# A recurrent spiking layer: TensorE's work of a time step gathered into two groups, each behind one wait

## The chip, the cores and the metric

The kernel runs on one core of a Trainium2 chip. The metric is the device time of one execution in microseconds (us), as the median of several runs. A core has five engines with instruction queues of their own: PE (TensorE, matrix products and transposes), DVE (VectorE), ACT (ScalarE), POOL (GpSimd) and SP (SyncE). They tell each other of finished work through semaphores: an instruction may wait for a semaphore to reach a value, and it may raise one when it has finished. DMA transfers raise semaphores too.

## The reference

A batch of 1024 sequences has 50 item numbers each. Every item has a row of 128 numbers in a table of 100,001 rows, and item 0 counts as a row of zeros. Per step t, the running sum of the rows is divided by min(t, length), normalized over the batch, and fed to a leaky neuron that fires at 1. The share of steps in which it fired, times the whole table transposed, is the output: 1024 x 100,001 scores.

```python
emb = emb_table.at[0].set(0.0)
prefix = jnp.cumsum(emb[seq], axis=1)
uF = prefix / denom[:, :, None]              # denom = min(t, length)
y = (uF - mean) * lax.rsqrt(var + BN_EPS) * gamma + beta   # mean, var over the batch
def step(v, x):
    v = v + (x - v) / TAU
    spike = atan_spike(v - V_TH)             # 1 where v >= V_TH
    return v - spike * V_TH, spike
_, spikes = lax.scan(step, v0, jnp.moveaxis(y, 1, 0))
scores = spikes.mean(axis=0) @ emb.T
```

## The kernel before

The kernel has two halves, and the order of the instructions of each engine is the order in which the program writes them.

**The scan** runs over the 50 steps. The 128 features lie on the partitions and the 1024 sequences along the free dimension, in two halves of 512 (h = 0 and 1)[...]. For step t, POOL gathers the 1024 rows with eight indirect DMAs of 128 rows (`gather`, L192 to L204) into a buffer `e`. A gather has its own one of eight DMA semaphores (the n-th of a step the n-th). Seven buffers take turns until step 42, three of them named `e` and four in the place where the second half's first two pairs of table slices will lie; the last seven steps use the three `e` buffers. `gathers` (L207) issues as many gathers as have a buffer whose earlier contents were read.

PE keeps the running sum of all rows in two PSUM banks, `pre[0]` and `pre[1]`. It adds a step by transposing the eight gathered blocks into them, four a bank (L313). `correct` (L269, matmuls on L271) subtracts row 0 of the table where the item is 0; it needs a small matrix `l` that ACT makes (`only`, L266). `counted` (L280, matmuls on L282) adds the spikes `s` of a step to two more banks, `sums`.

DVE scales each half of the sum to `uF` as soon as its four transposes are in (L322), takes statistics (L323, L333), finds the spikes of the step before (`s`, L343), and works out the normalization (L346 to L352). ACT applies it (L338, L356). DVE makes `negv` (L365) and the new potential `v` (L359). The scan's order on PE, for one step, is: four transposes of half 0, four of half 1, both corrections of the next step, both counts of the step before. In steps 42 and 44, `prepare` (L134) also transposes and splits the first two slices of the table, with a copy `hi` on ACT (L142) and a difference `lo` on DVE (L143). The last step takes its spikes with two DVE instructions ahead of `uF` (L307, L308).

**The product** (from L381) multiplies the counts, split into eight blocks of 128 sequences, by the table in slices of 1024 rows. The 36 slices that it needs first were fetched at the very start. Results go from PSUM through DVE (L472) and ACT (L474) to output buffers, and out by DMA from SP's queue: 409.6 MB.

Semaphores are set by the layer that records the program. Where instructions of one engine follow each other and only the last one's end has to be known, it may let one of them carry the increments of all. An instruction that must wait for more semaphores than it can hold gets wait instructions (EventSemaphore) in front of it.

Of the kernel before, what the change touches and what calls it, by code (L numbers as in the profile page):

```python
# [17 lines left out]
AF = mybir.ActivationFunctionType  # L18
ALU = mybir.AluOpType

P = 128
# [4 lines left out]
BANK = 512  # L26
# [8 lines left out]
def rec_kernel(  # L35
# [9 lines left out]
    nc = tc.nc  # L45
    B, T = seq.shape
    N, D = table.shape
    NB = B // P
# [18 lines left out]
    ident = const.tile([P, P], F32, tag="ident", name="ident")  # L67
# [10 lines left out]
    def pair(i):  # L78
        free.append([embp.tile([P, HALF], F32R, tag=f"{x}{i}", name=f"{x}_{i}") for x in ("hi", "lo")])
# [54 lines left out]
    def prepare(q, pt):  # L134
        turned(q, pt)
        split[q] = hi, lo = free.pop(0)
        hw = size(q)
        if hw % 2:
            nc.vector.memset(hi[:, hw : hw + 1].bitcast(F32), 0.0)
            nc.vector.memset(lo[:, hw : hw + 1].bitcast(F32), 0.0)  # L140
        vp, vh, vl = views(q, pt, hi, lo)
        nc.scalar.copy(vh, vp)  # L142
        nc.vector.tensor_tensor(vl, vp, vh.bitcast(F32), ALU.subtract)  # L143
# [18 lines left out]
    with ExitStack() as ph:  # L162
# [25 lines left out]
        slots += [f"e{(t - flat + 1) % 3}" for t in range(flat, T)]  # L188
        es = {}
        held = {}  # L190

        def gather(t):  # L192
            tag = slots[t]
            pool = gp if tag[0] == "e" else embp
            es[t] = pool.tile([P, B], F32, tag=tag, name=f"e_{t}")
            held[tag] = t
            for n in range(NB):
                nc.gpsimd.indirect_dma_start(  # L198
                    out=es[t][:, n * P : (n + 1) * P],
                    out_offset=None,  # L200
                    in_=table,
                    in_offset=bass.IndirectOffsetOnAxis(ap=idx[:, n, t : t + 1].bitcast(U32), axis=0),
                )
# [3 lines left out]
        def gathers(t):  # L207
            nonlocal to_gather
            while to_gather < T and held.get(slots[to_gather], -1) < t:
                gather(to_gather)  # L210
                to_gather += 1
# [4 lines left out]
        while slots[to_gather] != "e1":  # L216
            gather(to_gather)
            to_gather += 1
# [11 lines left out]
        r0n = once.tile([P, D], F32, tag="r0n", name="r0n")  # L230
# [3 lines left out]
        sel = once.tile([P, P // 2], F32, tag="sel", name="sel")  # L234
# [10 lines left out]
        rlen = once.tile([P, B], F32, tag="rlen", name="rlen")  # L245
# [14 lines left out]
        pre = [accp.tile([P, BANK], F32, tag=f"pre{h}", name=f"pre{h}") for h in range(B // BANK)]  # L260
        sums = [accp.tile([P, BANK], F32, tag=f"sums{h}", name=f"sums{h}") for h in range(B // BANK)]

        def only(t):

            l = sp.tile([P, D], F32R, tag="l", name=f"l_{t}")
            nc.scalar.activation(l, r0n, AF.Copy, scale=sel[:, t : t + 1])  # L266
            return l

        def correct(t, l):  # L269
            for h in range(B // BANK):  # L270
                nc.tensor.matmul(  # L271
                    pre[h],
                    lhsT=l,
                    rhs=zT[:, h * BANK : (h + 1) * BANK],
                    start=t == 0,
                    stop=False,
                    skip_group_check=True,
                )

        def counted(t, s):  # L280
            for h in range(B // BANK):
                nc.tensor.matmul(  # L282
                    sums[h],
                    lhsT=ident_h,
                    rhs=s[:, h * BANK : (h + 1) * BANK],
                    start=t == 0,
                    stop=t == T - 2,
                    skip_group_check=True,
                )
# [6 lines left out]
        halves = [slice(h * BANK, (h + 1) * BANK) for h in range(B // BANK)]  # L296
        v = None

        correct(0, only(0))
        l = only(1)  # L300
        for t in range(T):
            last = t == T - 1
            gathers(t)
            e = es.pop(t)
            if last:
                s = lp.tile([P, B], BF16, tag="s", name=f"s_{t - 1}")
                nc.vector.tensor_single_scalar(s, v, V_TH, ALU.is_ge)  # L307
                nc.vector.tensor_tensor(negv, s, v, ALU.subtract)  # L308
            uF = up.tile([P, B], F32, tag="uF", name=f"uF_{t}")
            bs = sp.tile([P, B // BANK, 6], F32, tag="bs", name=f"bs_{t}")  # L310
            for h, cs in enumerate(halves):
                for k in range(0, BANK, P):
                    nc.tensor.matmul(  # L313
                        pre[h][:, k : k + P],
                        lhsT=e[:, h * BANK + k : h * BANK + k + P],
                        rhs=ident,
                        start=False,
                        stop=last,
                        is_transpose=True,
                        skip_group_check=True,  # L320
                    )
                nc.vector.scalar_tensor_tensor(uF[:, cs], rlen[:, cs], 1.0 / (t + 1), pre[h], ALU.max, ALU.mult)  # L322
                nc.vector.bn_stats(bs[:, h, :], uF[:, cs])  # L323
            if not last:
                correct(t + 1, l)
            else:

                counted(t - 1, s)
                count = once.tile([P, B], F32, tag="zT", name="count")
                for h, cs in enumerate(halves):  # L330
                    nc.scalar.copy(count[:, cs], sums[h])
            mv = sp.tile([P, 2], F32, tag="mv", name=f"mv_{t}")
            nc.vector.bn_aggr(mv, bs.rearrange("p h s -> p (h s)"))  # L333


            r = sp.tile([P, 1], F32, tag="r", name=f"r_{t}")
            nc.scalar.activation(r, mv[:, 1:2], AF.Sqrt, bias=eps)  # L337
            nc.scalar.activation(uF, uF, AF.Identity, bias=mv[:, 0:1], scale=-1.0)  # L338


            if t and not last:
                s = lp.tile([P, B], BF16, tag="s", name=f"s_{t - 1}")
                nc.vector.tensor_single_scalar(s, v, V_TH, ALU.is_ge)  # L343
                counted(t - 1, s)

            nc.vector.reciprocal(r, r)  # L346
            q = sp.tile([P, 1], F32, tag="q", name=f"q_{t}")
            nc.vector.tensor_mul(q, r, r)
            nc.vector.scalar_tensor_tensor(q, mv[:, 1:2], BN_EPS, q, ALU.add, ALU.mult)
            nc.vector.tensor_scalar(q, q, -0.5, 1.5, ALU.mult, ALU.add)  # L350
            a = sp.tile([P, 1], F32, tag="a", name=f"a_{t}")
            nc.vector.tensor_scalar(a, q, r, hgb[:, 0:1], ALU.mult, ALU.mult)  # L352


            def x(vt, cs):
                nc.scalar.activation(vt, uF[:, cs], AF.Identity, bias=hgb[:, 1:2], scale=a)  # L356

            def step(vt, cs):
                nc.vector.scalar_tensor_tensor(vt, negv[:, cs], -0.5, vt, ALU.mult, ALU.add)  # L359

            if not last:
                vt = vp.tile([P, B], F32, tag=f"v{t % 2}", name=f"v_{t}")
                x(vt, whole)
                if t:
                    nc.vector.tensor_tensor(negv, s, v, ALU.subtract)  # L365
                step(vt, whole)
                v = vt
                if t + 2 < T:
                    l = only(t + 2)

                if t in (T - 8, T - 6):
                    q = (t - T + 8) // 2
                    pair(q)
                    prepare(q, vp.tile([P, HALF], F32, tag="v1", name=f"pt_{q}"))
# [15 lines left out]
        cs, vt, first = groups[0]  # L390
# [37 lines left out]
    for c, W in enumerate(WIDTHS):  # L428

        if c in (0, NARROW, MIDDLE):  # L430
# [3 lines left out]
            if c == 0:  # L434
                third = [op.tile([P, HALF], F32R, tag=x, name=x) for x in ("hi2", "lo2")]
                free.append(third)
                turns = [(op, f"o{k}", 2) for k in range(4)]
            elif c == NARROW:
                assert third in free
                free.remove(third)  # L440
                turns = [(op, f"o{k}", 3) for k in (2, 0, 1)]
            else:
                fourth = op.tile([P, 4, HALF], F32R, tag="pairs", name="pairs")
                free.extend((fourth[:, k, :], fourth[:, k + 1, :]) for k in (0, 2))
                turns = [(rowp, "rows2", 6), (rowp, "rows3", 6), (op, "o", 6)]
# [68 lines left out]
```

## Time and profile before

| | |
|---|---|
| median of 3 runs | 1676.47 us (1675.02 to 1677.37) |
| the profiled execution | 1672.07 us, of which the span in the trace is 1670.3 us |
| PE busy | 1111.4 us, 67% |
| DVE busy | 940.2 us, 56% |
| ACT busy | 630.7 us, 38% |
| POOL busy | 378.6 us, 23%, all of it in the first 586 us |
| DMA queue of the outputs (q1) | 428.77 MB |
| gathers (q0) | 26.24 MB in 400 indirect DMAs |
| first product of the second half | 604.34 us after the span's start |

All times in the text are us from the span's start unless it says otherwise. A busy time is the time in which an engine worked; a share of the span is a mean over both halves, so the halves have to be looked at apart. The start of a matmul is recorded, its end is modelled. The trace also holds the times at which each semaphore went up, though not every one of them, and each DMA packet. A row of a timeline gives the start, the duration, the engine, the line, the operation, what it writes and reads, and in brackets the engine's idle time before it and what ended that.

### The profile page before, as it was taken

Reading aid. Unit: us, or ns where it says so; the run is one execution under the profiler, and the core shown is the slowest. Engines: PE = TensorE matmul, PEld = TensorE weight load, DVE = VectorE, ACT = ScalarE, POOL = GpSimd, SP = SyncE. Lnnn points to the kernel's source line nnn. Section 1 sums busy time; section 2 is a strip of 40 time slices with the busy share of each in tenths; the row PEclk is TensorE's granted clock in tenths of the full one; section 3 lists DMA queues with packets and bytes.
Section 4 is the critical chain, followed back from the end, with each engine's and each line's share of the span. In section 5 each row is a group of like instructions: output and inputs, shape, how many; then the busy total and the mean of one; then the engine's idle time right before and its main releaser. Section 6 shows DMA issues by size and latency. Waiting matters only on the chain.

```text
span 1670.3 us, 12572 instructions
## 1 busy us (share of the span) xinstructions
PE 1111.4 (67%) x4548; PEld 830.0 (50%) x4548; DVE 940.2 (56%) x1161; ACT 630.7 (38%) x700; POOL 378.6 (23%) x406
## 2 busy tenths in 40 slices
PE   4113343434344479889988788878788888878785
PEld 2002121212222256666766666667666666666664
DVE  4225675657687875666655555555555554555553
ACT  2012232222232345545544444444444444444442
POOL 7766666667645600000000000000000000000000
PEclk9997555555555579999999999998999999999998
DMA  9511111111111149999999999999999999999998
GB/s 344 213 43 43 44 49 46 47 46 48 48 30 38 48 164 417 410 422 401 422 427 428 430 423 429 427 421 425 420 430 412 411 427 427 421 423 410 403 422 352
DMA packets 53691, 488.14 MB, mean 292 GB/s; under 512 B 11995, under 2 KB 12796, under 8 KB 32380
## 3 DMA queue, kind: packets, MB, share of 16 engines
q1 hardware_dynamic: 31984, 428.77, 61.1%
q0 software_dynamic: 12800, 26.24, 5.8%
q10 hardware_dynamic: 8844, 32.33, 4.9%
q8 instruction: 36, 0.59, 0.1%
q14 instruction: 27, 0.22, 0.0%
HBM read 77.69 MB, written 409.60 MB: 292 GB/s over the span
## 4 chain that ended last, share of the span: by engine, by line
DMA 48%; DVE 20%; another core or an unknown queue 11%; PE 9%; ACT 5%; issue 4%; POOL 2%; DVEq 0%; ACTq 0%; SPq 0%; POOLq 0%
DMA scores<-o 47%; PE po L150 8%; ACT o L474 4%; DVE bs L323 4%; DVE uF L322 3%; DVE v L359 3%; DVE s L343 3%; DVE negv L365 2%; POOL e L198 2%; DVE o L472 2%; DMA e<-in_L_rec_emb_table,idx 1%; DVE a L352 1%; ACT v L356 1%; DVE mv L333 1%
## 5 line engine op out<-in xcount | busy, mean ns | idle before, releaser
L472 DVE TENSOR_SCALAR o<-po 128x1024 f32<-128x1024 f32 x391 | 463.7, 1221 | 353.3 <-DMA scores<-o 320.6
L474 ACT ACTIVATE o<-po 128x1024 f32<-128x1024 f32 (+1 forms) x391 | 388.0, 1019 | 549.6 <-DMA scores<-o 344.2
L198 POOL DMA_INDIRECT e<-in_L_rec_emb_table,idx x400 | 377.9, 945 | 206.8 <-issue 113.3
L150 PE MATMUL po<-pairs,countB 128*128 128x512 f32 x1168 | 315.3, 416 | 65.2 <-ACT o L474 50.2
L150 PEld LDWEIGHTS po<-pairs,countB 128*128 128x128 f32 x1168 | 226.2, 199 | 130.8 <-ACT o L474 65.3
L150 PE MATMUL po<-pairs,countC 128*128 128x512 f32 x876 | 238.6, 418 | 44.7 <-ACT o L474 44.6
L271 PE MATMUL pre<-zT,l 128*128 128x512 f32 x100 | 75.3, 755 | 290.1 <-DVE uF L322 236.4
L150 PEld LDWEIGHTS po<-pairs,countC 128*128 128x128 f32 x876 | 169.2, 199 | 91.2 <-ACT o L474 56.2
L271 PEld LDWEIGHTS pre<-zT,l 128*128 128x128 f32 x100 | 28.0, 281 | 331.6 <-issue 217.6
L322 DVE SCALAR_TENSOR_TENSOR uF<-rlen,pre 128x512 f32<-128x512 f32 x100 | 67.9, 679 | 195.8 <-remote 173.7
L337 ACT ACTIVATE r<-mv,eps 128x1 f32<-128x1 f32 x50 | 14.7, 295 | 394.0 <-DVE mv L333 252.4
L143 DVE TENSOR_TENSOR pairs<-pt,pairs 128x1024 fp32r<-128x1024 f32 (+1 forms) x73 | 88.3, 1217 | 94.4 <-ACT pairs L142 94.3
L120 PE MATMUL pt<-ident,rows 128*128 128x128 f32 x782 | 111.6, 290 | 7.7 <-ACT o L474 3.6
L120 PEld LDWEIGHTS pt<-ident,rows 128*128 128x128 f32 x782 | 101.0, 152 | 28.2 <-issue 9.7
L313 PE MATMUL pre<-ident,e 128*128 128x128 f32 x400 | 99.6, 421 | 11.6 <-DMA e<-in_L_rec_emb_table,idx 9.7
L313 PEld LDWEIGHTS pre<-ident,e 128*128 128x128 f32 x400 | 86.1, 226 | 38.7 <-issue 24.1
L150 PE MATMUL po<-hi,countB 128*128 128x512 f32 x200 | 83.3, 416 | 18.4 <-ACT o L474 14.0
L282 PE MATMUL sums<-s,ident_h 128*128 128x512 bf16 x98 | 49.1, 604 | 63.9 <-issue 36.2
L150 PE MATMUL po<-lo,countB 128*128 128x512 f32 x200 | 81.1, 405 | 0.0
L150 PE MATMUL po<-pairs,countA 128*128 128x512 f32 (+1 forms) x292 | 73.5, 393 | 10.9 <-ACT o L474 10.8
L142 ACT CAST pairs<-pt 128x1024 fp32r<-128x1024 f32 (+1 forms) x73 | 73.6, 1008 | 14.6 <-PE pt L120 14.2
L150 PE MATMUL po<-hi,countC 128*128 128x512 f32 x150 | 62.8, 419 | 16.2 <-ACT o L474 16.1
(76 smaller groups left out, 849.5 us busy)
## 6 DMA issues: line engine op xcount, KB each, us to landing
scores<-o SPq DMA_DIRECT2D x96, 3072.0 KB
scores<-o SPq DMA_DIRECT2D x32, 1536.0 KB
rows<-in_L_rec_emb_table ACTq DMA_DIRECT2D x20, 1536.0 KB
scores<-o SPq DMA_DIRECT2D x22, 1024.0 KB
rows<-in_L_rec_emb_table SPq DMA_DIRECT2D x6, 3072.0 KB
scores<-o SPq DMA_DIRECT2D x8, 2048.0 KB
scores<-o SPq DMA_DIRECT2D x8, 1872.5 KB
e<-in_L_rec_emb_table,idx POOLq DMA_INDIRECT x400
```

What stands on the lines that cost most here:

```text
L120: nc.tensor.transpose(pt[:, k0 : k0 + kw], r[:kw, k0 : k0 + D], ident[:kw, :kw])
L142: nc.scalar.copy(vh, vp)
L143: nc.vector.tensor_tensor(vl, vp, vh.bitcast(F32), ALU.subtract)
L150: nc.tensor.matmul(po[:, :kw], lhsT=counts[n], rhs=part[:, k0 : k0 + kw], start=j == 0, stop=j == 1,)
L198: nc.gpsimd.indirect_dma_start(out=es[t][:, n * P : (n + 1) * P], out_offset=None, in_=table, in_offset=bass.IndirectOffsetOnAxis(ap=idx[: ...
L271: nc.tensor.matmul(pre[h], lhsT=l, rhs=zT[:, h * BANK : (h + 1) * BANK], start=t == 0, stop=False, skip_group_check=True,)
L313: nc.tensor.matmul(pre[h][:, k : k + P], lhsT=e[:, h * BANK + k : h * BANK + k + P], rhs=ident, start=False, stop=last, is_transpose=True, ...
L322: nc.vector.scalar_tensor_tensor(uF[:, cs], rlen[:, cs], 1.0 / (t + 1), pre[h], ALU.max, ALU.mult)
L323: nc.vector.bn_stats(bs[:, h, :], uF[:, cs])
L343: nc.vector.tensor_single_scalar(s, v, V_TH, ALU.is_ge)
L472: nc.vector.tensor_scalar_mul(o[:, h0 : h0 + hw], po[:, :hw], 1.0 / T)
L474: nc.scalar.mul(o[:, h0 : h0 + hw], po[:, :hw], 1.0 / T)
```

## The change

The transposes, corrections and counts of a step become one list, `summed(t, ready, spikes)`. It holds, in this order on PE: the counts that are due, the two corrections, the four transposes of half 0 (together the front group), then the four transposes of half 1 (the back group). `needs` gives the first instruction of the front group a dependency on all that the group needs: the matrix `l`, the reading of the second half of the last `uF`, and the first four gathers. The first instruction of the back group gets one on the other four gathers.

`summed(t + 1, ...)` is called in step t after both halves of `uF` are scaled. The spikes of step t - 1, found later in step t, are handed on in `spikes` and counted in step t + 1. In the last two steps it differs: the group of step 49 is written after the spikes of step 47 are found, counts two steps' spikes, and has no added dependencies. `gathers(t + 1)` instead of `gathers(t)` is called at the head of a step, since the transposes of step t are already written by then. What is computed stays the same.

```diff
@@ gather
             for n in range(NB):
-                nc.gpsimd.indirect_dma_start(
+                brought[t, n] = nc.gpsimd.indirect_dma_start(
...
+        def needs(ins, others):
+            for other in others:
+                tc.add_manual_dep(
+                    ins.ins,
+                    other.ins.name,
+                    mybir.DependencyInfo(mybir.DependencyClass.Sync, mybir.DependencyReason.DATA),
+                    reason="one wait in front of a group",
+                )
+
         def only(t):
-
             l = sp.tile([P, D], F32R, tag="l", name=f"l_{t}")
-            nc.scalar.activation(l, r0n, AF.Copy, scale=sel[:, t : t + 1])
-            return l
+            return l, nc.scalar.activation(l, r0n, AF.Copy, scale=sel[:, t : t + 1])
...
-        correct(0, only(0))
-        l = only(1)
+        def turns(t, h):
+            for k in range(0, BANK, P):
+                yield nc.tensor.matmul(
+                    pre[h][:, k : k + P],
+                    lhsT=es[t][:, h * BANK + k : h * BANK + k + P],
+                    rhs=ident,
+                    start=False,
+                    stop=t == T - 1,
+                    is_transpose=True,
+                    skip_group_check=True,
+                )
+
+        def summed(t, ready, spikes):
+            l, made = only_next.pop(t)
+            half = NB // 2
+            front = [ins for x in spikes for ins in counted(*x)] + list(correct(t, l)) + list(turns(t, 0))
+            back = list(turns(t, 1))
+            if t < T - 1:
+                needs(front[0], [made, *ready, *(brought[t, n] for n in range(half))])
+                needs(back[0], [brought[t, n] for n in range(half, NB)])
+            es.pop(t)
+
+        only_next = {t: only(t) for t in range(2)}
+        spikes = []
+        summed(0, [], [])
         for t in range(T):
             last = t == T - 1
-            gathers(t)
-            e = es.pop(t)
+            gathers(t + 1)
...
             for h, cs in enumerate(halves):
-                for k in range(0, BANK, P):
-                    nc.tensor.matmul(
...
-                nc.vector.scalar_tensor_tensor(uF[:, cs], rlen[:, cs], 1.0 / (t + 1), pre[h], ALU.max, ALU.mult)
+                scaled = nc.vector.scalar_tensor_tensor(
+                    uF[:, cs], rlen[:, cs], 1.0 / (t + 1), pre[h], ALU.max, ALU.mult
+                )
                 nc.vector.bn_stats(bs[:, h, :], uF[:, cs])
-            if not last:
-                correct(t + 1, l)
-            else:
-
-                counted(t - 1, s)
+            if t < T - 2:
+                summed(t + 1, [scaled], spikes)
+                spikes = []
+            elif last:
+                list(counted(t - 1, s))
...
                 nc.vector.tensor_single_scalar(s, v, V_TH, ALU.is_ge)
-                counted(t - 1, s)
+                spikes.append((t - 1, s))
+                if t == T - 2:
+                    summed(t + 1, [], spikes)
...
                 if t + 2 < T:
-                    l = only(t + 2)
+                    only_next[t + 2] = only(t + 2)
```

In `correct` and `counted`, `nc.tensor.matmul(` becomes `yield nc.tensor.matmul(`.

More of the change, by code (lines that the diff above doesn't have):

```diff
@@ L190, in rec_kernel @@
         held = {}
+        brought = {}
         def gather(t):
@@ L281, in counted @@
             for h in range(B // BANK):
-                nc.tensor.matmul(
+                yield nc.tensor.matmul(
                     sums[h],
@@ L297, in rec_kernel @@
         v = None
-        correct(0, only(0))
-        l = only(1)
+        def turns(t, h):
+            for k in range(0, BANK, P):
+                yield nc.tensor.matmul(
+                    pre[h][:, k : k + P],
[18 more added lines that the diff above has]
+        summed(0, [], [])
         for t in range(T):
             last = t == T - 1
-            gathers(t)
-            e = es.pop(t)
+            gathers(t + 1)
             if last:
@@ L311, in rec_kernel @@
             for h, cs in enumerate(halves):
-                for k in range(0, BANK, P):
[L313 to L322, printed above, removed]
-                nc.vector.bn_stats(bs[:, h, :], uF[:, cs])
-            if not last:
-                correct(t + 1, l)
-            else:
-                counted(t - 1, s)
+                scaled = nc.vector.scalar_tensor_tensor(
+                    uF[:, cs], rlen[:, cs], 1.0 / (t + 1), pre[h], ALU.max, ALU.mult
+                )
+                nc.vector.bn_stats(bs[:, h, :], uF[:, cs])
+            if t < T - 2:
[3 more added lines that the diff above has]
+                list(counted(t - 1, s))
                 count = once.tile([P, B], F32, tag="zT", name="count")
```

## The prediction

> **What bounds the kernel now.** I read the slices first. In the page's section 2, each digit is the tenth of 41.8 us in which an engine was busy:
>
> ```profile
> DVE  4225675657687875666655555555555554555553
> POOL 7766666667645600000000000000000000000000
> DMA  9511111111111149999999999999999999999998
> ```
>
> The kernel has two halves. From about 604 us on, DMA is full (99% there by the table of stretches, at 415 GB/s); that half takes 1066 us and moves as a block if it starts earlier. Before 604 us, in the scan of 50 steps, no engine is full: DVE has about 6 tenths, POOL 6 or 7, DMA 1. So the scan is bound by waits. Who waited for whom, 0 to 600 us (total us, times, longest):
>
> ```profile
> DVE uF L322 <- remote: 173.7, 29, 16.1
> POOL e L198 <- issue: 113.3, 372, 0.3
> POOL e L198 <- remote: 62.8, 16, 8.1
> POOL e L198 <- PE pre L313: 24.7, 1, 24.7
> ```
>
> "Remote" is a wait whose releaser the profile can't name. DVE loses 174 us of the scan in front of uF, which needs PE's transposes. Is it the gathered rows that are late? The timeline says no (start, duration; in brackets the idle time before):
>
> ```profile
> 303.70 1.91 PE L313 MATMUL pre<-ident,e 128*128 128x128 f32 x8
> 305.13 1.23 DVE L359 SCALAR_TENSOR_TENSOR v<-negv,v 128x1024 f32<-128x1024 f32 x1 [0.21 <-DVE negv L365]
> 306.58 0.94 POOL L198 DMA_INDIRECT e<-in_L_rec_emb_table,idx  x1 [0.30 <-issue]
> 312.54 0.69 DVE L322 SCALAR_TENSOR_TENSOR uF<-rlen,pre 128x512 f32<-128x512 f32 x1 [6.18 <-remote]
> 318.84 0.69 DVE L322 SCALAR_TENSOR_TENSOR uF<-rlen,pre 128x512 f32<-128x512 f32 x1 [4.88 <-remote]
> 319.07 0.95 POOL L198 DMA_INDIRECT e<-in_L_rec_emb_table,idx  x1 [4.06 <-remote]
> 322.44 1.91 PE L313 MATMUL pre<-ident,e 128*128 128x128 f32 x8
> 325.01 0.68 DVE L322 SCALAR_TENSOR_TENSOR uF<-rlen,pre 128x512 f32<-128x512 f32 x1
> ```
>
> This is step 21, then 22. The eight transposes of 21 stand at 303.7 to 305.6, 54 us after their rows landed (packets of step 21 end at 250.0), yet uF starts at 312.54 and 318.84. Step 22 does the same work with no wait. The trace's records of PE's own semaphore explain it: in 22 it goes up every 0.21 us; in 21 at 305.52, 307.63, 310.42, 312.52, 315.33, 317.42, 318.12 and 318.82, whole multiples of 0.70 us. At step 43 nothing arrives from 534.6 on, then nine updates come between 543.21 and 543.48, 0.035 us apart; no transpose (0.21 us) can run so fast. So PE has done the work and its signals are held back. Held steps are 2 to 5 (18 to 34 us a step), 8, 11, 13, 16, 18, 21, 24, 26, 29, 31, 34, 43, partly 37 and 45. In steps 38 to 40, where POOL pauses (24.7 us), none is held. A free step takes 7.48 us.
>
> POOL comes next. A gather is issued every 1.25 us, so a step's eight take 9.99 us, slower than a free step. POOL stops only when the slot of seven steps ago isn't read out: 62.8 + 24.7 us, each time behind a held step (319.07 right after 318.84).
>
> [...]
>
> **The change, part by part.**
> *Waits and signals.* In the built programs a step of before has each transpose wait for its own gather and signal by itself: eight, two from the corrections, one from the counts, eleven signals. After, the first four transposes carry one signal, so do the last four, and counts and corrections share one: three. Over the scan PE's signals fall from 533 to 151, at least 0.85 us apart. The waits become separate wait instructions, three before the first group and two before the second, against one: 4 x 0.05 us (the recorded length of the one before L271) = 0.2 us on PE a step.
> *PE's order.* A step's chain now starts when uF's second half is read. Waits 0.15; two counts 0.38 + 0.43 (starts 302.89, 303.27, 303.70); two corrections 0.6 each (300.83 to 301.43); four transposes, first to last start 0.64, and 0.65 from start to signal: 3.5 us to the first half; 0.1 + 0.85 more to the second, 4.4. DVE comes for the halves 5.5 us (300.78 to 306.27) and 6.8 us after that read. So the order costs nothing while DVE's own work covers it. Uncovered, it would be up to 4.4 us a step. Counts of two steps ago are read one step later; s has two buffers and is rewritten after that, so no new wait.
> *If signals flow, POOL sets the pace.* Step 0 takes 10.21 us (4.11 to 14.32) and 49 steps 9.99: the last gather ends at 14.32 + 489.5 - 0.3 = 503.5 us and lands 1.26 later (585.93 to 587.19 now), 504.8. PE's first group waits for the fourth gather, 5.0 us before the eighth: 3.5 us fits. The second group ends 0.1 + 0.64 + 0.65 = 1.4 us after the eighth. DVE then needs 6.2 us to the next uF and has 2.5 us to spare a step. POOL waits for no slot: it is one or two steps ahead, not seven.
> *prepare* (steps 42, 44) now has its PE transposes behind the next step's second group, so behind a landing: 1.05 + 1.7 + 0.5, hi 1.0 (L142), lo 1.23 (L143) = 5.5 us, then uF, bn, uF: 6.9 after the landing, not 1.4, so 5.5 us late. At 2.5 us a step that is gone by step 48.
> *The last step*, as before: uF's second half at 590.01 in step 48 and 600.02 in step 49, 10.0 apart by DVE's s and negv (L307, L308). New: 494.8 + 1.4 = 496.2, so 506.2, past the landing's 505.5.
> *Sum.* These two rows of the chain of waits carry the end:
>
> ```profile
> 600.02 0.60 DVE uF L322
> 604.34 2.05 PE sums L150 x4
> ```
>
> 600.0 - 506.2 = 93.8 us earlier, and everything after moves along. Span 1670.3 - 93.8 = 1576.5; the execution lasted 1672.1, so 1578.3. Its time lies 4.4 us under the median, 1676.5; held steps vary from run to run, so I carry over about half: **1581 us**.
>
> Unknown: what is left of the hold. From below, none. From above, each of three signals waits like those of step 21 (2.1 to 2.8 us). The first two lie on uF's first half (5 us), the third on the second. If they come due one after the other, DVE reads the second half about 3.4 us later than above; POOL's slack swallows 2.5 us a step until the end. I take none, plus up to 20 us upward.
>
> **Rivals.**
> *The hold shrinks but beats the slack.* If every signal waits 2.45 us in turn, 7.4 us on the 4.4 us chain, a held step is 12.4 us; with 45% held (16 of steps 2 to 37), 0.45 x 12.4 + 0.55 x 9.99 = 11.1, 1.1 us over POOL's pace: 45 steps, 50 us, about 1631. For it: nothing shows that sparse signals are safe; steps 0 and 1, with signals 1.2 us apart, were free, which speaks against.
> *Nothing happens.* The waits for gather semaphores cause the hold, and eight a step remain: about 1676. Against: the flush, which shows finished work. For: wherever a hold is seen, such waits came just before.
> *Slower.* PE now runs right at a landing in every step, when 16 increments arrive, and not in a lucky half of the steps. If each step is held as step 21 was (11.3 us), a step is 18.7 us where now uF goes from step 2 to step 37 in (488 - 45)/35 = 12.7: 35 x 6 = +210, about 1885; it decides above 12.7 us a step, a hold of 5.2 us in every step. For it: steps 2 to 4 were held for 18 to 26 us each, with fewer than seven steps landed ahead.
>
> **How the numbers follow.** POOL-bound scan 0.70 (1568 to 1602); smaller hold 0.11 (1602 to 1660); nothing happens 0.05; slower 0.14 (1690 to 1890). The first two hold 0.81, so the range is 1568 to 1660; the likeliest alone 1568 to 1602. A measurement tells about 0.2%, 3.4 us (runs lie from 1675.0 to 1677.4): faster 0.82, the same 0.03, slower 0.15.
>
> **What would show it.** Right: POOL has no long pauses, its gathers end near 503 us; DVE's "remote" wait before uF is gone or is named as a gather's, near 2.5 us a step; uF of the last step near 506; DMA full from about 510. PE's semaphore goes up three times a step and never in 0.70 us multiples. Wrong: multiples of 0.70 us between PE's signals; POOL waiting for slots; uF over 1.4 us behind the landing in most steps; or gathers slower than 1.25 us.

## The result: 0.7% slower, with the held signals still there

| | before | after |
|---|---|---|
| median | 1675.99 us (1675.02 to 1677.37, 4 runs) | 1687.46 us (1687.04 to 1691.60, 4 runs) |
| ratio, 95% interval | | 1.0073 [1.0056, 1.0091] |
| span of the profiled execution | 1670.3 us | 1685.3 us |
| last gather ends | 585.93 us | 596.74 us |
| `uF`, second half of step 45 | 567.22 us | 582.45 us |
| `uF`, second half of step 49 | 599.93 us | 614.97 us |

The forecast was 1581 us. The slices of the changed kernel (tenths of 42.1 us, as in the prediction) look like those of before:

```profile
DVE  4225666556667586556755555555555555555553
POOL 6756666666635510000000000000000000000000
DMA  9511111111111129999999999999999999999998
```

No engine is full before slice 15, and the product begins later, not earlier. The list of waits from 0 to 600 us (total, times, longest) tells the same:

```profile
DVE uF L342 <- remote: 182.7, 26, 16.2
POOL e L199 <- remote: 63.0, 13, 9.9
POOL e L199 <- PE pre L309: 35.4, 4, 24.9
ACT hi L142 <- remote: 25.8, 2, 15.2
```

DVE's wait in front of `uF`, 173.7 us before, is 182.7 us. POOL's pauses went from 62.8 + 24.7 to 63.0 + 35.4 us. The row of `hi` has grown: two waits, one of them 15.2 us, where the list of before has one:

```profile
ACT hi L142 <- remote: 11.6, 1, 11.6
```

The timeline shows a held step (20), the end of the hold, and then step 45 (start, duration; idle time before it in brackets):

```profile
289.92 0.67 DVE L342 SCALAR_TENSOR_TENSOR uF<-rlen,pre 128x512 f32<-128x512 f32 x1
292.36 1.91 PE L309 MATMUL pre<-ident,e 128*128 128x128 f32 x8
...
303.87 0.94 POOL L199 DMA_INDIRECT e<-in_L_rec_emb_table,idx  x1 [0.30 <-issue]
304.74 0.69 DVE L342 SCALAR_TENSOR_TENSOR uF<-rlen,pre 128x512 f32<-128x512 f32 x1 [8.56 <-remote]
308.96 0.69 DVE L342 SCALAR_TENSOR_TENSOR uF<-rlen,pre 128x512 f32<-128x512 f32 x1 [2.81 <-remote]
309.20 0.94 POOL L199 DMA_INDIRECT e<-in_L_rec_emb_table,idx  x1 [4.38 <-remote]
...
563.39 1.80 PE L120 MATMUL pt<-ident,rows 128*128 128x128 f32 x8 [0.61 <-DVE negv L389]
...
578.94 1.01 ACT L142 CAST hi<-pt 128x1024 fp32r<-128x1024 f32 x1 [15.19 <-remote]
579.98 1.23 DVE L143 TENSOR_TENSOR lo<-pt,hi 128x1024 fp32r<-128x1024 f32 x1 [15.30 <-ACT hi L142]
581.12 0.68 DVE L342 SCALAR_TENSOR_TENSOR uF<-rlen,pre 128x512 f32<-128x512 f32 x1
582.45 0.67 DVE L342 SCALAR_TENSOR_TENSOR uF<-rlen,pre 128x512 f32<-128x512 f32 x1
```

The eight transposes of step 20 stand at 292.4 to 294.3, with their rows long landed. There are three signals in the whole step, as the change intended, and PE's semaphore goes up for them at 294.89, 304.71 and 308.94: 9.82 and 4.23 us apart, about 14 and 6 times 0.70 us. So having fewer signals doesn't shorten a hold. From step 8 to 35 every third step is held, about 19 us, and two free ones of 7.49 us follow: 34.0 us for three steps.

The second part of the timeline is where the kernel gets slower. The transposes of the table's slices (`pt`, L120) end at 565.2; `hi`, which reads them, starts at 578.94. In the kernel before they end at 561.12, and `hi` follows at once (then `uF`'s second half):

```profile
561.16 1.01 ACT L142 CAST hi<-pt 128x1024 fp32r<-128x1024 f32 x1 [1.62 <-issue]
567.22 0.67 DVE L322 SCALAR_TENSOR_TENSOR uF<-rlen,pre 128x512 f32<-128x512 f32 x1
```

Of the 15.0 us between the spans, 4.1 are there at step 43 (546.74 to 550.87), about as much as runs of one kernel differ, and 11.1 come in step 45.

### The profile page after: what moved, and what is told of

Read it like the earlier page. It is cut to its first block, busy times and chain, and to the rows that moved or that the text cites. A ratio compares the mean times of both kernels' runs of the same rounds, so it can differ in the third digit from the quotient of the medians.

```text
span 1685.3 us, 12758 instructions
## 1 busy us (share of the span) xinstructions
PE 1075.3 (64%) x4538; PEld 834.7 (50%) x4548; DVE 940.5 (56%) x1161; ACT 631.3 (37%) x700; POOL 378.3 (22%) x406
## 4 chain that ended last, share of the span: by engine, by line
DMA 44%; DVE 20%; another core or an unknown queue 12%; PE 12%; ACT 7%; issue 4%; POOL 0%; ACTq 0%; DVEq 0%; SPq 0%
DMA scores<-o 44%; PE po L150 11%; ACT o L498 4%; DVE bs L345 4%; DVE uF L342 4%; DVE v L383 3%; DVE s L365 3%; DVE negv L389 2%; DVE o L496 2%; ACT v L380 1%; DVE a L376 1%; ACT uF L360 1%; DVE mv L355 1%; PE pt L120 0%
## 5 line engine op out<-in xcount | busy, mean ns | idle before, releaser
L150 PEld LDWEIGHTS po<-pairs,countC 128*128 128x128 f32 x876 | 170.9, 201 | 93.3 <-ACT o L498 58.1
L290 PEld LDWEIGHTS <-ident_h 128*128 128x128 bf16 x98 | 7.1, 106 | 416.2 <-issue 416.2
L342 DVE SCALAR_TENSOR_TENSOR uF<-rlen,pre 128x512 f32<-128x512 f32 x100 | 67.9, 679 | 198.1 <-remote 182.7
L120 PE MATMUL pt<-ident,rows 128*128 128x128 f32 x782 | 111.4, 289 | 4.9 <-issue 2.2
L120 PEld LDWEIGHTS pt<-ident,rows 128*128 128x128 f32 x782 | 100.9, 152 | 24.5 <-issue 7.5
L309 PE MATMUL pre<-ident,e 128*128 128x128 f32 x400 | 93.9, 411 | 8.3 <-DMA e<-in_L_rec_emb_table,idx 8.3
L279 PE MATMUL pre<-zT,l 128*128 128x512 f32 x100 | 70.0, 801 | 10.0 <-ACT uF L360 4.0
L150 PE MATMUL po<-hi,countC 128*128 128x512 f32 x150 | 64.9, 433 | 15.3 <-ACT o L498 15.2
```

Source lines behind the costliest of these rows:

```text
L120: nc.tensor.transpose(pt[:, k0 : k0 + kw], r[:kw, k0 : k0 + D], ident[:kw, :kw])
L150: nc.tensor.matmul(po[:, :kw], lhsT=counts[n], rhs=part[:, k0 : k0 + kw], start=j == 0, stop=j == 1,)
L279: yield nc.tensor.matmul(pre[h], lhsT=l, rhs=zT[:, h * BANK : (h + 1) * BANK], start=t == 0, stop=False, skip_group_check=True,)
L290: yield nc.tensor.matmul(sums[h], lhsT=ident_h, rhs=s[:, h * BANK : (h + 1) * BANK], start=t == 0, stop=t == T - 2, skip_group_check=True,)
L309: yield nc.tensor.matmul(pre[h][:, k : k + P], lhsT=es[t][:, h * BANK + k : h * BANK + k + P], rhs=ident, start=False, stop=t == T - 1, is ...
L342: scaled = nc.vector.scalar_tensor_tensor(uF[:, cs], rlen[:, cs], 1.0 / (t + 1), pre[h], ALU.max, ALU.mult)
```

## The experiments

The same kernel before takes 1674.6 to 1677.8 us (medians) in some sittings, as on the chip of the result, and 1576.1 to 1576.2 in others. Each run below was made beside the kernel before, on one chip, and I write **1676 kind** and **1576 kind** for the two. I don't know whether this belongs to a chip or to a condition that passes; the chip numbered 11 was of the 1676 kind in one sitting and of the 1576 kind an hour later. A time that stands without a ratio is that of a single execution.

### On the 1576 kind: nothing is held, and the sum of the forecast comes out

**The order alone.** The change without its added dependencies:

```diff
-            if t < T - 1:
+            if False:
                 needs(front[0], [made, *ready, *(brought[t, n] for n in range(half))])
```

> The change without its added dependencies: the new order on PE (counts of two steps ago, corrections, transposes), but each transpose waits for its own gather and signals by itself again, eight signals a step. Theory A (number of signals and waits is no matter): as slow as the change, 1683 to 1692, held steps in the same places, step 45 held for about 20 us. Theory of the prediction (grouping of signals matters): differs from the change by over 8 us. If the grouping itself did harm (18.5 us waits in front of a group): near 1676.

Measured: 1576.38 us against 1576.19 for before, ratio 1.0002 [0.9993, 1.001], span 1574.5. Waits, 0 to 600 us, of this run:

```profile
POOL e L199 <- issue: 115.5, 379, 0.3
DVE uF L342 <- PE pre L309: 103.4, 44, 3.0
DVE lo L143 <- ACT hi L142: 14.4, 6, 6.3
ACT hi L142 <- PE pt L120: 11.5, 4, 6.4
```

There is no "remote" in front of `uF`: DVE waits for PE by name, at most 3.0 us. POOL issues at 9.99 us a step without a pause (at most 0.3 us between two gathers), the last gather ends at 503.50, and `uF`'s second half of step 49 starts at 505.75. The forecast had 503.5 and 506.2, and a span of 1576.5. The delay of `hi` and `lo` is there (steps 43 and 45 last 15.2 and 12.5 us) and is gone by step 48. All that the forecast said of a scan without holds is right; but the kernel before is as fast there. (No trace of the kernel before was kept on this kind; that nothing is held in it is inferred from its time.) The question of the expectation, what the grouping of signals does to the holds, can't be answered where there are none.

**Rows by plain DMAs.** The item numbers, and with them the right rows, are left out; rows come in the order of the table, from SP's queue or from POOL's:

```diff
-                nc.gpsimd.indirect_dma_start(
-                    out=es[t][:, n * P : (n + 1) * P], ...
+                at = (t * NB + n) * P
+                nc.sync.dma_start(out=es[t][:, n * P : (n + 1) * P], in_=table[at : at + P, :])
```

> The kernel before, with each gather replaced by a plain DMA of 128 consecutive table rows of the same size, issued by SP; the item numbers are left out, so the rows are not the sequences'. POOL has nothing to do in the scan; DMAs, buffers, waits and PE's signals stay as many. Theory A (POOL's own issuing holds PE's completions back): no held step, all steps at 7.48 us or at SP's pace, DVE's remote wait before uF near 0, scan end (uF of step 49) near 400 to 430 us, the whole near 1490. Theory B (the DMAs' 16 increments each, from whatever queue, hold PE): held steps stay, scan near 600. Theory C (PE's burst holds itself): held steps stay as well.

> As the run with SP's plain DMAs of consecutive rows (item numbers left out), but issued by POOL. It tells POOL's issuing apart from the indirect form. Theory A: held steps are there again wherever POOL issues for over some 10 us without a pause; if POOL issues a plain DMA faster than 1.25 us, it runs into its buffers sooner, pauses more, and fewer steps are held. If only the indirect form holds PE: no held step, scan end near 400 to 430 us.

Measured: 1503.14 and 1463.83 us. From step 2 to step 36 each step takes 7.48 to 7.49 us, DVE's pace; the 39 us between the two are there at the start (step 0's second `uF` begins at 55.4 and 15.8 us). With before at 1576.19 this says only that a scan without POOL's 9.99 us is DVE's.

**A pause of POOL in each step.** The first gather of a step waits for the last one of the step before to land:

```diff
+                if n == 0 and t:
+                    tc.add_manual_dep(brought[t, 0].ins, brought[t - 1, NB - 1].ins.name, ...)
```

> The kernel before, with the first gather of each step waiting until the last gather of the step before has landed: a pause of about 1 us for POOL in each step (the landing lag is 1.25 us, the usual gap 0.30). Theory A (a hold begins only when POOL has issued for some 10 us without a pause): no held step or nearly none, steps at POOL's pace of 9.99 + 1.0 = 11.0 us, last gather near 555 us, the whole near 1640. Rival (a pause must be the 2.8 to 4.3 us that are seen when POOL waits for a buffer, or pauses don't matter): held steps stay, POOL loses 50 us more only where it wasn't waiting anyway, the whole 1676 to 1700.

Measured: 1688.07 us, ratio 1.0709 [1.0691, 1.0727]. POOL's pause is 2.3 us, not the 1 us of the expectation, and a step takes 12.0, so where nothing is held this costs 112 us.

### On the 1676 kind: the change again, and where its 11 us are

> The change itself, beside the kernel before. Where the kernel before takes about 1676 us (held signals of PE): theory 1, the hold is a property of that chip and the change doesn't touch it, 1687 (ratio 1.007). Where the kernel before takes about 1576 us (no held signal, POOL issues at 9.99 us a step without a pause): theory 1, the same 1576.5 within 3 us, last gather near 503.5, uF's second half of the last step near 506. Theory 2, the change as a whole is dearer (its added waits cost time wherever it runs, 15 us as on the first chip): 1591 or so there, and the gathers end later than 503.5.

Measured: 1685.91 us against 1674.62, ratio 1.0066 [1.0048, 1.0084], as in the result.

**The table's transposes first.** In steps 42 and 44 the next step's groups are written after `prepare`, as in the kernel before (the counts that are due by then go with them):

```diff
-            if t < T - 2:
+            if t < T - 2 and t not in (T - 8, T - 6):
                 summed(t + 1, [scaled], spikes)
...
                 prepare(...)
+                summed(t + 1, [scaled], spikes)
```

> The change, with the table's first transposes (steps 42 and 44) ahead of the next step's two groups, as in the kernel before. Where before takes 1676 us: theory 1 (the 11 us by which the change is slower are these transposes, shut in behind a held group of step 45), about 1677; theory 2 (the loss is spread over the scan) about 1687. Where before takes 1576 us both theories expect 1576.5, as the 5.5 us of delay are recovered by step 48.

Measured: 1673.61 us, ratio 0.9995 [0.998, 1.001], beside the change's 1.0066. The waits of this run:

```profile
DVE uF L342 <- remote: 178.9, 27, 16.1
ACT hi L142 <- remote: 10.1, 1, 10.1
```

The wait of 15.2 us for `hi` is gone, and with it the whole loss; one of 10.1 us is left, as in before (11.6). The holds in front of `uF` are as long as ever. So the loss needs the new order of these two steps, under a hold; the other 48 steps neither gain nor lose.

**The order alone**, again:

> The change's order of PE's work without its added waits: signals per transpose as in the kernel before. Where before takes 1676 us: if the grouped signals make no difference to the hold, 1687 as the change, with the same 11 us at step 45; if grouping them shortened holds, more than 1690; if grouping them is what costs (each group's signal counts four, and comes at the end), about 1676. Where before takes 1576 us: 1576.5 again.

Measured: 1678.48 us, ratio 1.0018 [1.0006, 1.003]. Of the change's 11 us, about three are left by the ratio. Its waits:

```profile
DVE uF L342 <- remote: 170.9, 20, 16.1
ACT hi L142 <- remote: 18.4, 2, 9.6
```

DVE's "remote" in front of `uF` is 170.9 us, near the 173.7 of before and the 182.7 of the change, and `hi`'s longest wait is 9.6 us in place of 15.2. So whether the transposes of a step carry two signals or eight makes little difference to the holds in the scan. Of the expectation's cases the last comes nearest: the loss at step 45 takes the new order and the grouped signals (or the waits added with them) together. How these make that hold longer, the two runs don't show.

### What is held, and by what

**Single pauses of POOL.** As the pause above, in each second and in each third step only (`t % 2 == 0`, `t % 3 == 0`):

> The kernel before, and the first gather of each second step waits until the last gather of the step before has landed: POOL pauses some 2.3 us after each 16 gathers. Where before takes 1676 us: theory 1 (PE's signals are held only while POOL issues gathers without a pause of its own), no 0.70 us multiples, 24 pauses on 9.99 us a step, 2.3 x 24 = 55 us on 1576.5, about 1632. Theory 2 (the hold has nothing to do with POOL's issuing), 1676 or more, held steps as before. Theory 3 (16 gathers without a pause are enough for a hold), held steps remain, 1650 to 1700. Where before takes 1576 us all expect 1632.

> As the run before, with a pause in each third step (after 24 gathers). Where before takes 1676 us: theory 1 without a hold 16 x 2.3 = 37 us on 1576.5, about 1613; theory 3 says that 24 gathers, 30 us, are time enough for a hold to begin, as in the change, where held steps come every third: 1650 to 1690. Where before takes 1576 us: about 1613.

Measured: 1677.95 us, ratio 1.0015 [0.9999, 1.0032], and 1675.32, 1.0011 [0.9991, 1.0032], where 1632 and 1613 would be the time without holds. My theory 1, that a pause ends the danger, falls. Some holds ended within a pause (bursts at 301.67 and 369.65 in the first of the two), but new ones followed, and the total stayed as it was. That fits a limit on the mean.

**The limit.** The ends of holds give its size. Many holds end with a burst of PE's signals 0.035 us apart. Counting gathers from the first after one such burst to the next burst (from the records of PE's semaphore):

| kernel | first gather | burst | gathers | us for each |
|---|---|---|---|---|
| before | 4.11 | 138.58 | 96 | 1.401 |
| before | 139.01 | 172.52 | 24 | 1.396 |
| before | 172.84 | 487.60 | 224 | 1.405 |
| order alone | 184.24 | 228.92 | 32 | 1.397 |
| order alone | 229.35 | 274.02 | 32 | 1.396 |

Over these stretches it is 1.40 us a gather, twice 0.70, though a gather is issued in 1.25 us (three other stretches of before, of 16 to 24 gathers, give 1.38 to 1.40). Theory R: on the 1676 kind a gather leaves something behind that is done at 1.40 us each; once enough of it is outstanding, PE's signals trickle until all is done. After n gathers without a pause 0.15 n us are outstanding, which is why a hold outlasts POOL by 4.9 us after 32 gathers (178.89 to 183.81 in the order alone) and by 3.8 after 24 (168.68 to 172.52 in before). A hold doesn't begin at once: in the changed kernel DVE's wait begins 21.0 us after POOL's restart (275.2 to 296.2, 309.2 to 330.2), with 17 gathers issued, so that by my estimate from these numbers 2 to 3 us are outstanding by then. I can't say what it is; landings aren't late (from the end of an issue to the last packet of the gather the median is 1.25 us in before and 1.27 us in the run "POOL aside" below).

**Rows by SP**, on this kind:

> Rows in the order of the table, fetched by plain DMAs from SP's queue: the item numbers and with them the right rows are left out, POOL has nothing to do. Where before takes 1676 us: theory 1 (the hold comes with POOL's gathers), no held step and 1503 as where before takes 1576 us; theory 2 (the hold is PE's or the chip's own, whoever fetches), held steps, over 1600.

Measured: 1503.21 us, the time of the other kind, and no held step. Without POOL's gathers nothing is held.

**POOL aside.** Rows by SP as above (the right rows are left out), and POOL issues the gathers of 40 steps into four buffers that nobody reads:

```diff
+            for n in range(NB if t < 40 else 0):
+                nc.gpsimd.indirect_dma_start(out=aside[t % 4][:, n * P : (n + 1) * P], ...)
```

> The rows that PE adds come in the order of the table by plain DMAs from SP (the item numbers and the right rows are left out); beside them POOL issues the gathers of 40 steps into four buffers that nobody reads, so PE waits for no gather and POOL for nobody. Where before takes 1676 us: if POOL's issuing holds PE's signals by itself (theory R), held steps as long as POOL issues without a pause, to about 410 us, and free steps of 7.5 us after that: over 1600, up to 1765. If the hold needs PE's waits for the gathers' semaphores, no held step and about 1503. Where before takes 1576 us: about 1503.

Measured: 1811.04 us beside 1677.72 for before. Its slices (tenths of 45.2 us):

```profile
DVE  1121121221999998766575555555555555555553
POOL 7777777773000000000000000000000000000000
```

And `uF` on its timeline, held and then free:

```profile
314.17 0.69 DVE L323 SCALAR_TENSOR_TENSOR uF<-rlen,pre 128x512 f32<-128x512 f32 x1 [16.13 <-remote]
325.37 0.69 DVE L323 SCALAR_TENSOR_TENSOR uF<-rlen,pre 128x512 f32<-128x512 f32 x1 [9.78 <-remote]
...
465.77 0.68 DVE L323 SCALAR_TENSOR_TENSOR uF<-rlen,pre 128x512 f32<-128x512 f32 x1
467.10 0.67 DVE L323 SCALAR_TENSOR_TENSOR uF<-rlen,pre 128x512 f32<-128x512 f32 x1
```

DVE works a tenth or two of the time while POOL issues, and all of it afterwards. Steps 3 to 11 last exactly 33.60 us each, 48 times 0.70, and steps 13 to 36 7.48 each. No wait on PE is for a gather, and no engine is named for any wait of POOL's between its gathers. The burst comes at 452.06, 27 us after the last gather (425.01): 4.2 + 320 x 1.40 = 452.2. So the gathers alone hold PE's signals, and for as long as 1.40 us a gather says; the expectation let the holds end with POOL's issuing, near 410, and had 1765 us at most.

The same trace shows the 1.40 us a second time, on POOL itself. For 179 gathers it issues every 1.25 us; then its own instructions get longer:

```profile
227.00 0.95 POOL L199 DMA_INDIRECT aside_hi<-in_L_rec_emb_table,idx  x1 [0.31 <-issue]
228.25 1.91 POOL L199 DMA_INDIRECT aside_hi<-in_L_rec_emb_table,idx  x1 [0.30 <-issue]
231.01 1.24 POOL L199 DMA_INDIRECT aside_hi<-in_L_rec_emb_table,idx  x1 [0.85 <-issue]
```

From 227.00 to the start of the last gather, 424.07, there are 141 gathers, 1.398 us each. At 227.0 some 26 us are outstanding (4.2 + 178 x 1.40 - 227.0, an estimate), about 19 gathers. This is what one would see if a store were full and emptied at 1.40 us a gather; what store it is, the trace doesn't show.

**Pace.** If the mean is what counts, gathers issued slower than 1.40 us each, 11.2 us a step, should hold nothing. First the pause in each step, 12.0 us, on this kind:

> The wait for the landing in each step (12.0 us a step) where before takes 1676 us: theory R no held step and the same 1688 as where before takes 1576 us; theory S held steps and 1700 or more.

Measured: 1689.07 us, as on the other kind (1688.07). No held step. Then a pace nearer the limit: the first gather waits for the landing of the seventh or the eighth gather of the step before in turn:

```diff
+                if n == 0 and t:
+                    until = 4 if t < 5 else 7 - t % 2
+                    tc.add_manual_dep(brought[t, 0].ins, brought[t - 1, until].ins.name, ...)
```

> The kernel before, with POOL slowed evenly: the first gather of a step waits for the landing of the seventh or (every second step) the last gather of the step before, and in the first four steps of the fifth. POOL's step becomes some 11.4 us (12.0 and 10.8 in turn) in place of 9.99. Where before takes 1676 us: theory R (a gather leaves work behind that this chip does in 1.41 us, 11.28 us a step, and PE's signals stand behind what has piled up) no held step after the first few, last gather near 571, uF's second half of the last step near 574 in place of 600, 1649. Theory S (holds come whatever POOL's pace, and fill up whatever time is left) held steps, 1676 or more. Where before takes 1576 us both 1649.

Measured: 1650.84 us, ratio 0.9837 [0.9821, 0.9853], with 11.48 us a step. The waits of this run:

```profile
DVE uF L331 <- PE pre L322: 162.2, 66, 4.0
POOL e L199 <- PE pre L322: 59.7, 36, 3.4
POOL e L199 <- DMA e<-in_L_rec_emb_table,idx: 17.8, 10, 2.5
```

No row of `uF` has "remote"; none of DVE's waits for PE is over 4.0 us. No step is held; only at 512, 535 and 558 us do a few of PE's signals come in small bunches, after gaps of 2.1 to 3.5 us. POOL pauses as often as it was told to, and nowhere for 24 us as before. POOL issues more slowly and the scan ends 20 us earlier. The two other paces use `6 + (t % 3 == 0)` and `6` in place of `7 - t % 2`:

> As e9_paced, but the wait for the last gather only in each third step: 11.22 us a step, 1.40 us a gather. Where before takes 1676 us: theory R with 1.38 us of work left by each gather (the value that fits the ends of the holds so far) no held step, 44 x 0.26 = 11 us less than e9_paced, 1640. If the work is over 1.40 us a gather, held steps come back late in the scan and it takes 1645 to 1676.

> As e9_paced, with the wait for the seventh gather in every step: 10.8 us a step, 1.35 us a gather. Where before takes 1676 us: theory R with 1.38 us: POOL gets ahead by 0.24 us a step, so held steps come back, 1640 to 1680 and more than e11_pace_112. If the work is 1.35 us or less, no held step and 30 us less than e9_paced, 1621.

Measured: 11.22 us a step, 1673.17 us (1659.17 to 1685.97), ratio 0.9972 [0.9958, 0.9986]; its first steps are free and held ones begin about step 20. 10.8 us a step, 1683.20 us, ratio 1.0038 [1.0025, 1.0051]; held from step 8 on, and just above the 1680 us of the expectation. The expectation of 1640 for 11.22 missed: it took 1.38 us for a gather, and at 1.40 this pace has no margin. The limit lies between 11.22 and 11.48 us a step, or just at the former.

**The change, paced** as in the 1650.84 us run:

> The change with e9's pacing of POOL (11.48 us a step measured there). Where before takes 1676 us: theory R no held step, uF's second half of the last step near 580, 1650 as e9_paced, so that the change's order costs and brings nothing once nothing is held. Rival: the added waits lengthen the chain from a landing to uF and, through the slots, POOL's step: 1655 or more. Where before takes 1576 us the same.

Measured: 1650.15 us, ratio 0.9842 [0.9823, 0.986]. With no step held the change costs nothing and brings nothing. These two paced kernels are the only ones here with the whole computation that beat both before and after clearly, on the 1676 kind. On the other kind neither was run; there a pace of 11.48 us can be expected to cost time, as the 12.0 us did.

**Plain DMAs of POOL, for the limit.** Does any DMA of POOL do this, or the gather by item numbers? POOL fetches plain rows aside, or plain rows for PE (the right rows left out in both):

> As e8_pool_aside (PE's rows by SP in the table's order, the item numbers left out), but what POOL fetches aside for nobody are plain DMAs of 128 consecutive rows, the same bytes, some 0.55 us each to issue. Where before takes 1676 us: if any DMA of POOL leaves 1.40 us of work behind, 320 of them are cleared at 4 + 320 x 1.40 = 452 us, held steps of 33.6 us until then and about 1811 as e8_pool_aside; if it is the gather by item numbers, no held step and about 1503. Where before takes 1576 us: 1503.

> All rows by plain DMAs of POOL (in the table's order, the item numbers left out), POOL waiting for slots. Where before takes 1676 us: if any DMA of POOL leaves 1.40 us behind, 400 x 1.40 = 560 us for the scan with held steps, 1640 or more; if it is the gather by item numbers, 1464 as where before takes 1576 us.

Measured: 1528.12 and 1464.62 us, no held step; but before took 1576.12 beside them, so this was the kind on which nothing is held anyway, and the two tell nothing about the question. It stays open.

**Records that are missing.** The traces show one more difference between the kinds. Each gather has 16 packets of four bytes in the trace (6400 for the 400 gathers of before) and raises its semaphore as many times. On the 1576 kind the trace records nearly all of these raises (6394 in the order alone there). On the 1676 kind most are missing wherever POOL gathers: 1237 of 6400 are recorded in before, 1421 in after, 2105 in the paced kernel and 560 of 5120 in POOL aside. Of PE's semaphore too only about 300 updates are recorded in the scan of before, against about 550 in the order alone there. With the rows by SP the traces of both kinds have the same number of records of DMAs, 9692. In before the first gather after a burst (139.01, 172.84) has all 16 records, and soon most have 0 to 6. So what the gathers overrun may be the recording of the semaphores' updates, or a path that it shares. The executions timed here have a span and a clock on record, so they were recorded ones, and no run shows whether there are holds without a recording. That the signals themselves are late, and not only their records, is shown by DVE, which starts `uF` at 304.74, after 8.56 us of idle time, when the signal of 304.71 has come.

## Why the prediction was wrong

**The step that failed** is the one on what is left of the hold: "PE's signals fall from 533 to 151, at least 0.85 us apart" and then, of the hold, "I take none". It took the number of PE's signals for the cause, which no trace or run had shown. The signals are what is held, not what holds. With three a step instead of eleven the scan loses 182.7 us in front of `uF` instead of 173.7. With nobody waiting for a gather, POOL's gathers alone hold a step for 33.60 us; with gathers at 11.48 us a step no step is held, in the kernel before and in the changed one alike. The forecast's 1576.5 us is the time of a scan without the hold, and the kernel before takes it by itself (1576.19 us) where there is no hold.

**The sum that was there.** With 1.40 us a gather the scan of before can be added up: 4.1 + 400 x 1.40 = 564 us, plus 22.1 us at step 43 (487.6 to 509.7, when what was outstanding was done and POOL waited for a slot, since three buffers take the place of seven), plus 0.3 to 0.5 us at each of four other restarts: about 588, and the last burst begins at 588.50. The 1.40 us come from this trace, so this is a check and no forecast. The prediction had the key in its hand ("In steps 38 to 40, where POOL pauses (24.7 us), none is held") and used it for nothing. A pause of POOL in which PE's signals flow again should have led to the question what POOL does to PE.

**What bounds the scan**: "bound by waits", signals held while the work is done: right, and seen again in each run of that kind whose gathers aren't paced. "POOL comes next", 9.99 us a step: right only where nothing is held. There it gave 503.5 and 506.2, measured 503.50 and 505.75. On the 1676 kind the gathers count 11.2 us a step.

**The order of PE's work** costs nothing: right. Free steps are 7.49 us after the change as before; order alone has 1.0002 on the 1576 kind; the paced pair differs by 0.7 us.

***prepare***: "5.5 us late", "gone by step 48": right where nothing is held. Under a hold the transposes of the table stand behind a held group. `hi` started 13.8 us after they had ended. POOL gathered on until 577.15, without the pause that it makes from 563.41 to 566.26 in the kernel before, and the hold ended 1.8 us after it stopped; the step's 11 us weren't recovered. No rival had this: moving these transposes back takes away the whole loss (ratio 0.9995). The forecast priced the delay at a landing, 5.5 us, and not at a hold.

**The rivals.** "Nothing happens" named 1676, nearest to the result, but for a wrong reason: it blamed the waits for the gathers' semaphores, which POOL aside shows not to be needed. "Slower" ended on the right side by a mechanism that isn't there: PE doesn't run at the landing, since from step 4 to 36 POOL has issued five to six steps ahead. "The hold shrinks" is refuted by the 182.7 us; its sum was also off, as 4.4 + 7.4 is 11.8 us and not 12.4, which gives about 1618 and not 1631. Together they held 0.30, which was too little for a cause inferred from a coincidence: that PE's signals were dense and were late. No view had varied one without the other.

## What to carry to other kernels

When completions are late on one engine, vary what the other engines do before redesigning that engine's signals: a burst of late completions that comes whenever some queue has stopped for a while points to that queue. In before the six bursts of PE's signals come 2.4 to 6.9 us after the end of the last gather that POOL issued ahead of them. A producer that looks idle a quarter of the time (POOL is busy 0.94 of each 1.25 us) may already be over a limit on its mean rate; slowing POOL from 9.99 to 11.48 us a step made this kernel 1.6% faster where the limit existed. And measure the unchanged kernel in more than one sitting: here it alone differs by 100 us. Records that are missing from one trace and not from another are a sign worth following too.

## What the runs showed of the hardware

In these recorded executions PE's completions are held back by POOL's gathers: each gather of 128 rows of 512 bytes takes 1.25 us to issue, but on the 1676 kind its consequences last 1.40 us (1.38 to 1.405 over stretches of 16 to 320 gathers), and until they are worked off PE's semaphore rises at about whole multiples of 0.70 us (9.82 and 4.23 us in step 20 of the changed kernel), with a step of 33.60 us at the worst. The rows themselves land 1.25 us after the issue all the same, and PE's records show the matmuls starting at their usual times: in before the eight transposes start 3.59 us after the last `uF` in front of them in step 21, which is held, and 3.60 us in step 22, which is free. Whether the recording has a part in it is open.

Rows fetched by SP's DMAs hold nothing: on the 1676 kind they alone give 1503.21 us and no held step, and with POOL's gathers beside them 1811.04 us. What part of a gather takes the 1.40 us is shown by no run. Why the 1576 kind has no such limit, or one under 1.25 us, is open too.

In the traces of before and after no computing or DMA instruction waits for more than one semaphore by itself, and a wait instruction of PE for one or two. PE has 83 wait instructions in before and 278 in after.
